# Two transformer layers with a mixture of experts: the last layer norm moved from behind the twelfth expert to beside the eleventh

## The chip, the cores and the metric

The kernel runs on one core of one Trainium2 chip. The metric is the device time of one execution in microseconds (us), median over runs. The profile is one execution taken by the hardware profiler; its times count from the start of its span. Engines: PE is TensorE (matmuls; PEld is its weight load), DVE is VectorE, ACT is ScalarE, POOL is GpSimd, SP is SyncE, which here only issues DMAs. Each engine works through its own instructions in order.

## The reference

Four sub-layers on x of 4 x 1024 rows of 256 float32, each followed by a residual sum and a layer norm: attention with 16 heads, a gated feed-forward network, causal attention with 8 heads, and a mixture of 16 experts. Only the last of them and its norm matter for this change:

```python
logits = xn @ router_weight.T + router_bias
gate_vals, expert_idx = top_k(softmax(logits), 2)
# each expert takes at most CAP = 512 rows, in token order; rows over that are dropped
dispatch = zeros((16, CAP, 256)).at[e_flat, slot].add(xn[tok] * keep)
h = gelu(einsum('ech,efh->ecf', dispatch[4:], fc1) + fc1_bias)     # 12 experts with an MLP, 1024 wide
out_mlp = einsum('ecf,ehf->ech', h, fc2) + fc2_bias
# expert 0 gives zero, 1 its input, 2 and 3 a constant vector
combined = (expert_out[e_flat, slot] * w).sum over the 2 choices / gate_sums
x = layernorm(x + combined)
```

A row of the result therefore has its sum complete only when both experts that chose it are through, and a norm of a row needs the whole sum.

## The kernel before

Everything up to the experts is written out in one hand-made order: the block under `tc.manual_schedule()`, opened at the top and closed by `ordered.close()` (L1457), in which each engine gets its instructions in the order in which the program records them. From L1457 on the planner of the tile framework orders the instructions itself, by its own estimates of when inputs are there.

Tokens are held as 32 tiles of 128 rows (NT = 32, P = 128). Two DRAM tensors carry the mixture of experts. `disp_d` has 512 slots of 260 floats for each of the 12 MLP experts: 256 values of a row, then its expert, its two weights and its token's place, written by indirect DMAs on POOL. Empty slots hold zeros and a place from N = 4096 upwards. `acc_d` has 4096 + 512 rows of 256 floats: the residual plus what the cheap experts give is written there first (`base`, L872), and each MLP expert then adds its rows by an indirect DMA with addition (L1512); the 512 rows at the end take the empty slots. Row p of tile t lies in `acc_d` at place p * 32 + t, so one partition of the last stage reads four tiles as one run of 4 KB.

The loop over the 12 experts e (L1467 on) does for each: load the expert's 512 rows `dm` (four chunks of 128; `load_rows`, on SP's queue, after all rows of all tokens are sent); weights `w` of the rows (L1478, L1479); 8 transposes into `dmT` (L99, copies L100); first matmul `ph` in four PSUM pieces of two buffers (L1492) with the Gelu into `hTm` on ACT (L1500); second matmul `py` in four chunks c (L1508, two PSUM buffers); bias and weight on DVE into `yo` (L1509, L1510); scatter with addition into `acc_d` (L1512). Weights `f1`, `f2` have two buffers each and `load_expert` (L1376 and L1378) fetches them two experts ahead: f1 on SP's queue, f2 on ACT's.

When the last scatter has landed, the last norm begins. SP loads the 4096 rows as eight groups `xo` of four tiles (L1532, 512 KB each). For each group DVE takes the moments (`bn_stats`, `bn_aggr`, L1557 and L1558), POOL the inverse root (`inv_std`, L105 and L106) and the shift `sho` (L1561, L1562), ACT normalises three tiles (L1544) and DVE one (`normalise`, L110), and SP stores the group to `out` (L1550; the last group in two halves, L1548).

Of the kernel before, what the change touches and what calls it, by code (L numbers as in the profile page):

```python
# [19 lines left out]
P = 128  # L20
B, S, C = 4, 1024, 256
N = B * S
NT = N // P
# [12 lines left out]
def postln_layers_kernel(ctx: ExitStack, tc: tile.TileContext, a: dict, out: bass.AP):  # L36
# [29 lines left out]

    disp_d = dram.tile([NSLOT + 2 * N, ROW], F32, name="disp_d")
    acc_d = dram.tile([N + CAP, C], F32, name="acc_d")
    acc_rows = acc_d[0:N, :].rearrange("(p t) d -> p t d", t=NT)


    before = const.tile([P, P], F32, name="before")
# [8 lines left out]
    eidx = const.tile([P, E], F32, name="eidx")  # L81
    nc.vector.tensor_copy(eidx, eidx_i)
    tok_i = const.tile([P, NT], I32, name="tok_i")
    nc.gpsimd.iota(tok_i, pattern=[[1, NT]], base=0, channel_multiplier=NT)
    none_f = const.tile([P, 2, NT], F32, name="none_f")
    for k in range(2):
        nc.vector.tensor_scalar_add(none_f[:, k], tok_i, float(NSLOT + k * N))
# [21 lines left out]
    def normalise(x, mean, rs):  # L109
        nc.vector.tensor_scalar(x, x, mean, rs, ALU.subtract, ALU.mult)  # L110

    with ExitStack() as main:
# [614 lines left out]
        def dispatch(b, big, part=None):  # L727
# [20 lines left out]
            def choose(k):  # L748

                assert (b, (first + n) // 2 - 1) in routed  # L750
                lg = logits()
                if k == 0:
                    t = late_tile(b, [P, 2, ROW], F32, "xn", 12, f"oh_{name}").rearrange("p i d -> p (i d)")
# [83 lines left out]

            def staged(i):
                if ("st", i) not in v:
                    v["st", i] = late_tile(b, [P, 2, ROW], F32, "xn", 12, f"row_{name}_{i}")  # L840
                return v["st", i]

            def row(t):
# [610 lines left out]
        load_rows(0, dm0)  # L1454
        for step in sums3[1:] + sums:
            step()
        ordered.close()  # L1457


    ps_big = ctx.enter_context(tc.tile_pool(name="ps_ph", bufs=2, space=PSUM))  # L1460
# [2 lines left out]
    mo = ctx.enter_context(tc.tile_pool(name="mo", bufs=1))  # L1463


    added = [[]]
    rows = [dm0]  # L1467
    for e in range(EM):
        f1, f2 = loaded[e]
        dm = rows[e]  # L1470
        dmT = mo.tile([P, 2, CAP], F32, tag="dmT", bufs=2, name=f"dmT_{e}")
        hT = mo.tile([P, FF1 // P, CAP], F32, tag="hTm", bufs=2, name=f"hTm_{e}")
        if e + 1 < EM:
            rows.append(mo.tile([P, ECH, ROW], F32, tag="dm", bufs=2, name=f"dm_{e + 1}"))
            load_rows(e + 1, rows[-1])

        w = mo.tile([P, ECH], F32, tag="w", bufs=2, name=f"w_{e}")
        nc.vector.scalar_tensor_tensor(w, dm[:, :, C], float(e - EM), dm[:, :, C + 1], ALU.is_equal, ALU.mult)  # L1478
        nc.vector.tensor_tensor(w, w, dm[:, :, C + 2], ALU.add)  # L1479
        for c in range(2):  # L1480
            transpose_to(
                dmT[:, c, :].rearrange("p (n q) -> p n q", n=ECH),
                lambda i: dm[:, i, c * P : (c + 1) * P],
                ps_m,
                f"ptd_{e}_{c}",
                nc.any.tensor_copy if e else nc.scalar.copy,
            )
        for f in range(0, FF1 // P, 2):
            ph = ps_big.tile([P, S], F32, tag="big", name=f"ph_{e}_{f}")
            for i in range(2):  # L1490
                for c in range(2):
                    nc.tensor.matmul(  # L1492
                        ph[:, i * CAP : (i + 1) * CAP],
                        f1[:, c, (f + i) * P : (f + i + 1) * P],
                        dmT[:, c, :],
                        start=c == 0,
                        stop=c == 1,
                    )
            for i in range(2):
                nc.scalar.activation(  # L1500
                    hT[:, f + i, :], ph[:, i * CAP : (i + 1) * CAP], AF.Gelu, bias=b1[:, e, f + i : f + i + 1]
                )
        yo = mo.tile([P, ECH, C], F32, tag="yo", bufs=2, name=f"yo_{e}")
        added.append([])
        for c in range(ECH):
            py = ps_av.tile([P, 512], F32, tag="av", name=f"py_{e}_{c}")
            for f in range(FF1 // P):
                nc.tensor.matmul(py[:, :C], hT[:, f, c * P : (c + 1) * P], f2[:, f, :], start=f == 0, stop=f == FF1 // P - 1)  # L1508
            nc.vector.tensor_tensor(yo[:, c, :], py[:, :C], b2[:, e, :], ALU.add)  # L1509
            nc.vector.tensor_scalar_mul(yo[:, c, :], yo[:, c, :], w[:, c : c + 1])  # L1510

            ins = nc.gpsimd.indirect_dma_start(  # L1512
                out=acc_d,
                out_offset=bass.IndirectOffsetOnAxis(ap=dm[:, c, C + 3 : C + 4].bitcast(I32), axis=0),
                in_=yo[:, c, :],
                in_offset=None,
                compute_op=ALU.add,
            )
            for other in added[e + 1]:
                tc.declare_no_dep(ins.ins, other, reason="different rows")  # L1520
            for other in added[e] if e else based:
                tc.add_manual_dep(ins.ins, other.name, must, reason="the same rows")
            added[e + 1].append(ins.ins)
        if e + 2 < EM:
            loaded.append(load_expert(e + 2, nc.scalar))


    GRP = 4
    xo = []
    for t0 in range(0, NT, GRP):  # L1530
        x = mo.tile([P, GRP, C], F32, tag="xo", bufs=NT // GRP, name=f"xo_{t0}")
        ins = nc.sync.dma_start(x, acc_rows[:, t0 : t0 + GRP, :])  # L1532
        for other in added[EM]:
            tc.add_manual_dep(ins.ins, other.name, must, reason="all experts' rows")
        xo.append(x)
    done = []

    def finish(x, mv, rs, sh, t0):
        last = t0 + GRP == NT
        for t in range(GRP):  # L1540
            if t == GRP - 1 or (last and t % 2):
                normalise(x[:, t], mv[:, t, 0:1], rs[:, t : t + 1])
            else:
                nc.scalar.activation(x[:, t], x[:, t], AF.Identity, bias=sh[:, t : t + 1], scale=rs[:, t : t + 1])  # L1544
            if t % 2 and last:
                lo = t0 + t - 1
                eng = nc.sync if t == 1 else nc.scalar
                eng.dma_start(out[lo * P : (lo + 2) * P, :].rearrange("(t p) d -> p t d", p=P), x[:, t - 1 : t + 1])  # L1548
        if not last:
            nc.sync.dma_start(out[t0 * P : (t0 + GRP) * P, :].rearrange("(t p) d -> p t d", p=P), x)  # L1550

    for k, x in enumerate(xo):
        t0 = k * GRP
        mv = mo.tile([P, GRP, 2], F32, tag="mvo", bufs=4, name=f"mvo_{t0}")
        for t in range(GRP):
            st = mo.tile([P, 6], F32, tag="bnst", bufs=4, name=f"st_o_{t0 + t}")
            nc.vector.bn_stats(st, x[:, t])  # L1557
            nc.vector.bn_aggr(mv[:, t], st)  # L1558
        rs = inv_std(mo, mv[:, :, 1], GRP, f"o_{t0}")
        sh = mo.tile([P, GRP], F32, tag="sho", bufs=4, name=f"sho_{t0}")  # L1560
        nc.gpsimd.tensor_scalar(sh, mv[:, :, 0], -1.0, None, ALU.mult)  # L1561
        nc.gpsimd.tensor_tensor(sh, sh, rs, ALU.mult)  # L1562
        done.append((x, mv, rs, sh, t0))
        if len(done) > 1:
            finish(*done.pop(0))
    finish(*done.pop())


def _arrays(i):
# [61 lines left out]
```

## Time and profile before

| | |
|---|---|
| runs | 2420.87, 2433.54, 2437.45 us; median 2433.54 us |
| profiled execution | 2424.9 us, span 2423.2 us |
| mean granted TensorE clock | 0.967 |
| PE busy | 2300.8 us, 95% of the span |
| DVE, ACT, POOL busy | 1380.2, 1019.7, 737.5 us |
| DMA | 107.78 MB, 44 GB/s over the span |
| experts, first `ph` to last `py` | 2038.73 to 2388.26 us |
| behind the last `py` | 2388.26 to 2423.2 us |

The last row is the stage that the change is about; the row above it is the stage into which work is moved. Busy shares are means over the whole span, in which these two stages are 16%, so they say little about either.

### The profile page before, as it was taken

The numbers are of one execution on the slowest core, as the hardware profiler recorded it, in microseconds if no ns is written. First come the engines' busy times: TensorE is split into PE (matmuls) and PEld (weight loads), VectorE is DVE, ScalarE is ACT, GpSimd is POOL, SyncE is SP. The second block draws the span as 40 slices with busy tenths as digits, with TensorE's granted clock in tenths as the row PEclk, the third lists the DMA queues.
The fourth block names the chain that finished last, engine by engine and source line by source line (L and its number), as shares of the span: only waits on it lengthen the run. The fifth ranks groups of instructions, "written<-read, shape, count | busy, mean of one in ns | idle before, by whom it ended". The sixth has DMA issues, their size and how long they took to land.

```text
span 2423.2 us, 36155 instructions
## 1 busy us (share of the span) xinstructions
PE 2300.8 (95%) x14004; PEld 1138.6 (47%) x14004; DVE 1380.2 (57%) x3231; ACT 1019.7 (42%) x2039; POOL 737.5 (30%) x1101
## 2 busy tenths in 40 slices
PE   8999999999999999999999999999999985999994
PEld 5333334444444443444444434445556443666662
DVE  7766766666557476776674767717645774111113
ACT  2565665555543445545434555562332331111112
POOL 5335337223205143253241420211112153222223
PEclk9999999999999999999999999998999886999997
DMA  3234111000000000000100000112000012444434
GB/s 104 62 120 138 59 59 51 1 28 1 1 28 1 1 1 24 5 27 27 54 1 1 1 1 12 36 46 80 1 1 1 1 58 92 96 107 107 106 88 150
DMA packets 78125, 107.78 MB, mean 44 GB/s; under 512 B 8832, under 2 KB 67200, under 8 KB 76288
## 3 DMA queue, kind: packets, MB, share of 16 engines
q1 hardware_dynamic: 48592, 73.34, 9.3%
q0 software_dynamic: 9984, 14.82, 3.2%
q10 hardware_dynamic: 19376, 17.30, 2.3%
q8 instruction: 110, 1.80, 0.3%
q14 instruction: 63, 0.52, 0.1%
HBM read 66.54 MB, written 38.90 MB: 44 GB/s over the span
## 4 chain that ended last, share of the span: by engine, by line
PE 87%; DVE 8%; DMA 1%; issue 1%; ACT 1%; POOL 1%; SPq 0%; DVEq 0%; POOLq 0%; ACTq 0%
PE sc L491 21%; PE av L509 10%; PE ph L1492 7%; PE py L1508 7%; PE gu L655 7%; PE mx L960 5%; PE sc L1010 4%; PE mx L467 4%; PE p L929 4%; PE dn L671 3%; PE av L1047 3%; PE ppa L589 3%; PE dn L1047 2%; DVE masked L970 2%; PE qk L321 2%; PE pt L458 1%
## 5 line engine op out<-in xcount | busy, mean ns | idle before, releaser
L470 DVE TENSOR_REDUCE part<-mx 128x1 f32<-128x512 f32 x1024 | 655.6, 684 | 305.8 <-PE mx L467 300.8
L500 ACT ACTIVATE pe<-sc 128x512 f32<-128x512 f32 x1024 | 554.2, 596 | 392.4 <-PE mx L467 349.2
L467 PE MATMUL mx<-kT,qT 32*128 32x512 f32 x2048 | 621.6, 637 | 0.2 <-DVE part L470 0.2
L491 PE MATMUL sc<-qT,kT 32*128 32x512 f32 x2048 | 604.3, 637 | 0.0
L491 PEld LDWEIGHTS sc<-qT,kT 32*128 32x128 f32 x2048 | 176.0, 183 | 218.3 <-issue 174.5
L509 PE MATMUL av<-pe,va 128*32 128x512 f32 x2048 | 272.9, 605 | 0.0
L1021 ACT ACTIVATE pe<-sc 128x512 f32<-128x512 f32 (+3 forms) x384 | 157.3, 496 | 202.2 <-PE sc L1010 202.0
L467 PEld LDWEIGHTS mx<-kT,qT 32*128 32x128 f32 x2048 | 186.1, 183 | 33.3 <-issue 16.0
L970 DVE CUSTOM_DVE_ANT_0 masked<-mx,mask_w 128x128 bf16<-128x128 f32 (+3 forms) x256 | 125.4, 490 | 111.7 <-PE mx L960 82.0
L1492 PE MATMUL ph<-dmT,f 128*128 128x512 f32 x384 | 170.4, 602 | 6.8 <-DVE dmT L100 3.5
L1500 ACT ACTIVATE hTm<-ph,b 128x512 f32<-128x512 f32 x96 | 60.8, 684 | 262.2 <-PE ph L1492 262.2
L1508 PE MATMUL py<-f,hTm 128*128 128x256 f32 x768 | 167.7, 379 | 0.0
L1512 POOL DMA_INDIRECT acc_d<-yo,dm x48 | 74.6, 1554 | 287.0 <-DVE yo L1510 243.8
L1508 PEld LDWEIGHTS py<-f,hTm 128*128 128x128 f32 x768 | 145.9, 190 | 25.0 <-issue 5.7
L1024 POOL TENSOR_SCALAR_AFFINE_SELECT pe<-pe 128x256 f32<-128x256 f32 x128 | 51.7, 412 | 313.2 <-ACT pe L1021 311.5
L960 PE MATMUL mx<-kT,qT 32*128 32x512 f32 (+3 forms) x768 | 138.6, 578 | 3.4 <-DVE x L556 2.7
L1509 DVE TENSOR_TENSOR yo<-py,b 128x256 f32<-128x256 f32 x48 | 20.4, 425 | 213.1 <-PE py L1508 213.1
L386 POOL TENSOR_TENSOR ss<-ss,neg_half 128x16 f32<-128x16 f32 x48 | 139.3, 2910 | 0.5
L509 PEld LDWEIGHTS av<-pe,va 128*32 128x32 f32 x2048 | 40.4, 108 | 192.5 <-issue 186.4
L1010 PE MATMUL sc<-qT,kT 32*128 32x512 f32 (+3 forms) x768 | 123.7, 550 | 5.2 <-ACT pe L1021 1.5
L1492 PEld LDWEIGHTS ph<-dmT,f 128*128 128x128 f32 x384 | 72.9, 192 | 97.4 <-issue 86.8
L856 POOL DMA_INDIRECT disp_d<-row,si x48 | 48.4, 1009 | 221.6 <-DVE row L845 215.4
(350 smaller groups left out, 2992.7 us busy)
## 6 DMA issues: line engine op xcount, KB each, us to landing
f<-in_fc SPq DMA_DIRECT2D x14, 1024.0 KB, 5.0
f<-in_fc ACTq DMA_DIRECT2D x10, 1024.0 KB, 5.9
disp_d<-empty ACTq DMA_DIRECT2D x12, 520.0 KB, 3.3
xink<-in_xT SPq DMA_DIRECT2D x24, 256.0 KB, 3.0
qk_d<-xs SPq DMA_DIRECT2D x6, 1024.0 KB, 5.1
xr<-qk_d SPq DMA_DIRECT2D x6, 1024.0 KB, 6.0
dm<-disp_d SPq DMA_DIRECT2D x11, 520.0 KB, 3.6
x<-in_x SPq DMA_DIRECT2D x32, 128.0 KB, 2.7
```

What stands on the lines that cost most here:

```text
L467: nc.tensor.matmul(sc, self.qT[r, t * P : (t + 1) * P], self.kT[r, u * 512 : (u + 1) * 512], start=True, stop=True)
L470: return lambda: nc.vector.tensor_reduce(self.part[:, t, u, h : h + 1], sc, AX.X, ALU.max, negate=True)
L491: nc.tensor.matmul(sc, self.m.kT[r, kt * P : (kt + 1) * P], self.m.qT[r, qb * 512 : (qb + 1) * 512], start=True, stop=True)
L500: nc.scalar.activation(self.pes[i, h // 2][:, h % 2, :], sc, AF.Exp)
L509: nc.tensor.matmul(self.av[32 * h : 32 * h + 32, :], va0[:, kt, 4 * self.g + h, :], self.pes[i, h // 2][:, h % 2, :], start=kt == 0, stop= ...
L655: nc.tensor.matmul(ps[:, i * 256 : (i + 1) * 256], w[:, c, f * P : (f + 1) * P], xT[j][:, c, :], start=c == 0, stop=c == 1,)
L960: nc.tensor.matmul(scs[h][:, :n], qT[r, t * P : (t + 1) * P], kT[r, u * 512 : u * 512 + n], start=True, stop=True,)
L970: nc.vector.tensor_tensor_reduce(masked[:, :n], scs[h][:, :n], mask_w[:, 512 - n :], -1.0, -NEG, ALU.add, ALU.min, part)
L1010: nc.tensor.matmul(scs[h][:, off:], ones_h[r, :] if w else kT[r, kt * P : (kt + 1) * P], (self.m.nmT if w else qT)[r, q], start=w == 0, st ...
L1021: nc.scalar.activation(pe[:, j, off:], scs[2 * hp + j][:, off:], AF.Exp)
L1492: nc.tensor.matmul(ph[:, i * CAP : (i + 1) * CAP], f1[:, c, (f + i) * P : (f + i + 1) * P], dmT[:, c, :], start=c == 0, stop=c == 1,)
L1508: nc.tensor.matmul(py[:, :C], hT[:, f, c * P : (c + 1) * P], f2[:, f, :], start=f == 0, stop=f == FF1 // P - 1)
```

## The change

The norm of all rows no longer waits for the last expert. While expert 10 (the second last) runs, all 4096 rows are loaded from `acc_d`, with the sums of experts 0 to 9 in them, normed and stored to `out`. The rows that experts 10 and 11 still change are then handled apart: each of these two experts gathers its rows from `acc_d` by an indirect DMA into `xl`, adds its own share to them in SBUF, norms the 512 rows there, and scatters the normed rows over `out` (`place`). Expert 10 also adds its rows to `acc_d`, since expert 11 may share tokens with it. So that empty slots do no harm, `fill_empty` puts the row of the expert's first slot (`one`, read from `disp_d` into all partitions) and its place into every empty slot of experts 10 and 11.

Three further edits go with it. Rows lie in `acc_d` at their token's number, t * 128 + p, so that the same index serves `out`; a load of a group is then four runs of 1 KB for each partition. The experts stand in the hand-made order: `ordered.close()` moves to the end, each expert's rows are turned (`turn_rows`) ahead of the last `py` chunk of the expert before it, `load_expert(e + 1)` and `load_rows(e + 1)` stand after the first `ph` piece of expert e, and a small memset stands ahead of each scatter. `dmT` of expert 0 lies in the pool `tail`, whose tag `xn` has 10 buffers and not 12. All copies of `dmT` are on ACT; before, the planner placed them.

```diff
-    acc_rows = acc_d[0:N, :].rearrange("(p t) d -> p t d", t=NT)
+    acc_rows = acc_d[0:N, :].rearrange("(t p) d -> p t d", p=P)
...
-    nc.gpsimd.iota(tok_i, pattern=[[1, NT]], base=0, channel_multiplier=NT)
+    nc.gpsimd.iota(tok_i, pattern=[[P, NT]], base=0, channel_multiplier=1)
...
-                    v["st", i] = late_tile(b, [P, 2, ROW], F32, "xn", 12, f"row_{name}_{i}")
+                    v["st", i] = late_tile(b, [P, 2, ROW], F32, "xn", 10, f"row_{name}_{i}")
...
-        ordered.close()
...
+    def load_result(t0):
+        x = mo.tile([P, GRP, C], F32, tag="xo", bufs=NT // GRP, name=f"xo_{t0}")
+        ins = nc.sync.dma_start(x, acc_rows[:, t0 : t0 + GRP, :])
+        for other in added[EM - 2]:
+            tc.add_manual_dep(ins.ins, other.name, must, reason="the experts' rows")
+        return x
+    def moments(x, mv, name):
+        st = mo.tile([P, 6], F32, tag="bnst", bufs=4, name=f"st_o_{name}")
+        nc.vector.bn_stats(st, x)
+        nc.vector.bn_aggr(mv, st)
+    def statistics(x, t0):
...
+        for t in range(GRP):
+            moments(x[:, t], mv[:, t], t0 + t)
...
+        inv_std(mo, mv[:, :, 1], GRP, f"o_{t0}", rs)
...
+    def finish():
+        x, mv, rs, sh, t0 = normed.pop(0)
+        for t in range(GRP):
+            if t == GRP - 1:
+                normalise(x[:, t], mv[:, t, 0:1], rs[:, t : t + 1])
+            else:
+                nc.scalar.activation(x[:, t], x[:, t], AF.Identity, bias=sh[:, t : t + 1], scale=rs[:, t : t + 1])
+        to = out[t0 * P : (t0 + GRP) * P, :].rearrange("(t p) d -> p t d", p=P)
+        stored.append(nc.sync.dma_start(to, x).ins)
+    def fill_empty(e, dm):
+        one = mo.tile([P, ROW], F32, tag="one", bufs=1, name=f"one_{e}")
+        ins = nc.sync.dma_start(one, disp_d[e * CAP, :].partition_broadcast(P))
...
+        nc.vector.tensor_copy(first, one[:, C + 3 : C + 4].bitcast(I32))
+        nc.vector.tensor_scalar(first, first, float(N - 1), None, ALU.min)
+        nc.vector.tensor_copy(to, dm[:, :, C + 3].bitcast(I32))
+        nc.vector.tensor_scalar(gap, to, float(N), None, ALU.is_ge)
+        for c in range(ECH):
+            nc.vector.scalar_tensor_tensor(
+                dm[:, c, : C + 3], one[:, : C + 3], gap[:, c : c + 1], dm[:, c, : C + 3], ALU.mult, ALU.add
+            )
...
+        return to_i
...
+    def place(e, c):
+        nc.gpsimd.memset(spacer, 0.0)
+        ins = nc.gpsimd.indirect_dma_start(
+            out=out,
+            out_offset=bass.IndirectOffsetOnAxis(ap=to_is[e][:, c : c + 1], axis=0),
+            in_=xls[e][:, c, :],
+            in_offset=None,
+        )
+        for other in stored + placed[-1:]:
+            tc.add_manual_dep(ins.ins, other.name, must, reason="the rows' last form")
+        placed.append(ins.ins)
...
+    turn_rows(0)
     for e in range(EM):
+        if near:
+            xls[e] = mo.tile([P, ECH, C], F32, tag="xl", bufs=2, name=f"xl_{e}")
+            for c in range(ECH):
+                ins = nc.gpsimd.indirect_dma_start(
+                    out=xls[e][:, c, :],
+                    out_offset=None,
+                    in_=acc_d,
+                    in_offset=bass.IndirectOffsetOnAxis(ap=to_is[e][:, c : c + 1], axis=0),
+                )
+                for other in added[e]:
+                    tc.add_manual_dep(ins.ins, other.name, must, reason="the same rows")
+        if last:
+            for c in range(ECH):
+                place(e - 1, c)
+        if near and not last:
+            xo = [load_result(t0) for t0 in range(0, NT, GRP)]
         for f in range(0, FF1 // P, 2):
...
+            if f == 0 and not last:
+                if 0 < e:
+                    loaded.append(load_expert(e + 1, nc.scalar))
+                rows[e + 1] = mo.tile([P, ECH, ROW], F32, tag="dm", bufs=2, name=f"dm_{e + 1}")
+                load_rows(e + 1, rows[e + 1])
+        if e >= EM - 3 and not last:
+            to_is[e + 1] = fill_empty(e + 1, rows[e + 1])
+        if near and not last:
+            for k in range(5):
+                statistics(xo[k], k * GRP)
+                if k:
+                    finish()
...
         for c in range(ECH):
+            if c == ECH - 1 and not last:
+                turn_rows(e + 1)
...
+            if near:
+                x = xls[e][:, c, :]
+                if last:
+                    nc.vector.scalar_tensor_tensor(x, yo[:, c, :], w, x, ALU.mult, ALU.add)
+                else:
+                    nc.vector.tensor_tensor(x, yo[:, c, :], x, ALU.add)
+                mv = mo.tile([P, 2], F32, tag="mvl", bufs=2, name=f"mvl_{e}_{c}")
+                moments(x, mv, f"{e}_{c}")
+                rs = inv_std(mo, mv[:, 1:2], 1, f"l_{e}_{c}")
+                normalise(x, mv[:, 0:1], rs)
+                if last:
+                    place(e, c)
+                elif c < 3:
+                    statistics(xo[5 + c], (5 + c) * GRP)
+        while normed:
+            finish()
+    ordered.close()
```

More of the change, by code (lines that the diff above doesn't have):

```diff
@@ L752, in choose @@
                 if k == 0:
-                    t = late_tile(b, [P, 2, ROW], F32, "xn", 12, f"oh_{name}").rearrange("p i d -> p (i d)")
+                    t = late_tile(b, [P, 2, ROW], F32, "xn", 10, f"oh_{name}").rearrange("p i d -> p (i d)")
                     for i, key in enumerate((("oh", 0), ("oh", 1), "both", "cum")):
@@ L1463, in postln_layers_kernel @@
     mo = ctx.enter_context(tc.tile_pool(name="mo", bufs=1))
+    GRP = 4
+    stored, normed = [], []
+    def load_result(t0):
[8 more added lines that the diff above has]
+        nc.vector.bn_aggr(mv, st)
@@ new lines, in statistics @@
+    def statistics(x, t0):
+        mv = mo.tile([P, GRP, 2], F32, tag="mvo", bufs=NT // GRP, name=f"mvo_{t0}")
+        for t in range(GRP):
+            moments(x[:, t], mv[:, t], t0 + t)
+        rs = mo.tile([P, GRP], F32, tag="rso", bufs=NT // GRP, name=f"rs_o_{t0}")
+        inv_std(mo, mv[:, :, 1], GRP, f"o_{t0}", rs)
+        sh = mo.tile([P, GRP], F32, tag="sho", bufs=NT // GRP, name=f"sho_{t0}")
+        nc.gpsimd.tensor_scalar(sh, mv[:, :, 0], -1.0, None, ALU.mult)
+        nc.gpsimd.tensor_tensor(sh, sh, rs, ALU.mult)
+        normed.append((x, mv, rs, sh, t0))
@@ new lines, in finish @@
+    def finish():
[10 more added lines that the diff above has]
+        ins = nc.sync.dma_start(one, disp_d[e * CAP, :].partition_broadcast(P))
+        for other in sent:
+            tc.add_manual_dep(ins.ins, other.name, must, reason="rows of all tokens")
+        to, gap, away = [mo.tile([P, ECH], F32, tag=n, bufs=1, name=f"{n}_{e}") for n in ("to", "gap", "away")]
+        first = mo.tile([P, 1], F32, tag="first", bufs=1, name=f"first_{e}")
+        to_i = mo.tile([P, ECH], I32, tag="to_i", bufs=2, name=f"to_i_{e}")
+        nc.vector.tensor_copy(first, one[:, C + 3 : C + 4].bitcast(I32))
[6 more added lines that the diff above has]
+            )
+        nc.vector.tensor_scalar(away, to, first, -1.0, ALU.subtract, ALU.mult)
+        nc.vector.tensor_tensor(away, away, gap, ALU.mult)
+        nc.vector.tensor_tensor(to_i, to, away, ALU.add)
+        return to_i
@@ L1466, in postln_layers_kernel, with turn_rows @@
     added = [[]]
-    rows = [dm0]
-    for e in range(EM):
-        f1, f2 = loaded[e]
+    rows, dmTs, ws = {0: dm0}, {}, {}
+    def turn_rows(e):
         dm = rows[e]
[L1471 to L1477, printed above, removed]
+        pool, tag = (mo, dict(tag="dmT", bufs=2)) if e else (tail, {})
+        dmTs[e] = dmT = pool.tile([P, 2, CAP], F32, name=f"dmT_{e}", **tag)
+        ws[e] = w = mo.tile([P, ECH], F32, tag="w", bufs=2, name=f"w_{e}")
@@ L1485, in postln_layers_kernel @@
                 f"ptd_{e}_{c}",
-                nc.any.tensor_copy if e else nc.scalar.copy,
+                nc.scalar.copy,
             )
+    placed = []
+    def place(e, c):
[9 more added lines that the diff above has]
+        placed.append(ins.ins)
+    to_is, xls = {}, {}
+    turn_rows(0)
+    for e in range(EM):
+        last = e == EM - 1
+        near = e >= EM - 2
+        f1, f2 = loaded[e]
+        dm, dmT = rows[e], dmTs[e]
+        hT = mo.tile([P, FF1 // P, CAP], F32, tag="hTm", bufs=2, name=f"hTm_{e}")
+        if near:
[14 more added lines that the diff above has]
+            xo = [load_result(t0) for t0 in range(0, NT, GRP)]
         for f in range(0, FF1 // P, 2):
@@ L1508, in postln_layers_kernel @@
                 nc.tensor.matmul(py[:, :C], hT[:, f, c * P : (c + 1) * P], f2[:, f, :], start=f == 0, stop=f == FF1 // P - 1)
+            w = ws[e][:, c : c + 1]
             nc.vector.tensor_tensor(yo[:, c, :], py[:, :C], b2[:, e, :], ALU.add)
[L1510 to L1565, printed above, removed]
@@ L1566, in postln_layers_kernel @@
-    finish(*done.pop())
+            if not last:
+                nc.vector.tensor_scalar_mul(yo[:, c, :], yo[:, c, :], w)
+                nc.gpsimd.memset(spacer, 0.0)
+                ins = nc.gpsimd.indirect_dma_start(
+                    out=acc_d,
+                    out_offset=bass.IndirectOffsetOnAxis(ap=dm[:, c, C + 3 : C + 4].bitcast(I32), axis=0),
+                    in_=yo[:, c, :],
+                    in_offset=None,
+                    compute_op=ALU.add,
+                )
+                for other in added[e + 1]:
+                    tc.declare_no_dep(ins.ins, other, reason="different rows")
+                for other in added[e] if e else based:
+                    tc.add_manual_dep(ins.ins, other.name, must, reason="the same rows")
+                added[e + 1].append(ins.ins)
```

## The prediction

> **What bounds the kernel now.** I read the chain that ended last first, in order of time, then the windows around its end. The chain is PE for 87% of the span, and from 2038.73 on it is one expert behind the other: 14.0 us of `ph`, 13.8 us of `py`, every 29.0 us. Behind the last `py` it leaves PE for good.
>
> ```profile
> 2038.73 16.37 PE ph L1492 x32
> ...
> 2360.43 14.00 PE ph L1492 x32
> 2374.43 13.83 PE py L1508 x64
> 2389.37 3.80 DMA acc_d<-yo,dm
> 2393.32 4.04 DMA xo<-acc_d
> ```
>
> ```profile
> 2302.00:2331.00 29.00, 28.66 (x106) 19.09 (x104) 4.60 (x13) 5.06 (x8) 6.20 (x4) 1.00 0.44 109
> 2388.30:2423.20 34.90, 0.00 (x0) 0.00 (x0) 17.28 (x75) 12.17 (x23) 14.89 (x33) 0.55 0.73 248
> ```
>
> The columns of a window are PE, PEld, DVE, ACT and POOL busy, the clock, the DMA share and GB/s. During one expert (first row) PE is full and DVE has 24 us free. The tail of 34.9 us (second row) has no PE at all: 5.1 us until the last scatter has landed, 4.1 until the first group is in, 20 of norms, the rest stores. That tail is what the change can win. It would need DVE to fit the norms beside the eleventh expert without PE noticing.
>
> **What comes off and what stays as a tail.** I count from T, the start of `ph` of expert 10 (2331.50 before); the span before ends at T + 91.7. The new tail behind the last `py`, on one chunk: handoff 0.2, bias 0.42, weight and sum 0.48 (the row of L870, the same kind of DVE operation), moments 0.43 and 0.2, inverse root on POOL about 1.0, norm 0.41, handoffs 0.2, an indirect write 2.6 from issue to landing (the row of `disp_d<-row,si`), and the 2.6 us that lie before between the landing of the last store (issued 2417.70, 2.9 to land) and the span's end: 8.5 us in place of 34.9. With no stall the end would be T + 57.8 + 8.5 = T + 66.3, a gain of 25.4.
>
> **The stall that the program order makes.** It is read from where the instructions stand. On SP the eight `xo` loads now stand ahead of three others: f1 of expert 11, `dm` of expert 11 and `one` of expert 11. On DVE `fill_empty(11)`, which waits for `dm` and `one`, stands ahead of all statistics and of all four `yo` of expert 10. So everything that DVE does in expert 10 waits until SP's queue has worked off the 4 MB. Before, `dm` was never behind more than one weight load, and no `yo` stood behind it.
>
> When does `one` land? The last scatter of expert 9 releases the first `xo` load 5.1 us after PE's end (2388.26 to 2393.32), here at T + 5.1. Then these have to pass: `xo` 4.19 MB, f2 of expert 11 on ACT's queue (1.05, issued about T + 5.1 behind the first Gelu pair), four gathers (0.52), f1 (1.05), `dm` (0.53), `one` (0.13): 7.48 MB. Three rows for the rate, and one for the order:
>
> ```profile
> 2395.00:2405.00 10.00, 0.00 (x0) 0.00 (x0) 7.25 (x33) 3.16 (x6) 4.69 (x11) 0.50 1.00 401
> ...
> 2331.50:2333.00 1.50, 1.50 (x4) 0.78 (x5) 0.81 (x2) 0.00 (x0) 1.02 (x1) 1.00 0.78 162
> 2333.00:2334.50 1.50, 1.50 (x5) 0.65 (x4) 0.00 (x0) 0.00 (x0) 0.53 (x1) 1.00 1.04 371
> ```
>
> ```profile
> dm<-disp_d SPq DMA_DIRECT2D x11, 520.0 KB, 3.6
> ```
>
> ```profile
> DMA to landing us min/median/max: 2.4/4.2/9.4
> ```
>
> The first row is the `xo` load in runs of 4 KB (401 GB/s), the third an f2 load in runs of 1 KB once it streams (371), the second its beginning beside a scatter (162). The changed `xo` load has runs of 1 KB, so I take 380 GB/s: 19.7 us. The first `xo` landed 4.06 us after its issue, of which 1.3 are its own bytes, so 2.8 us are fixed. `one` lands at T + 5.1 + 2.8 + 19.7 = **T + 27.6**. By the HBM limit of 358 GB/s for a core (the Trainium skill, "DMA: Bandwidth & Descriptors", Specifications) it would be 20.9 us and T + 28.8; the rows are above that limit, so I stay with them.
>
> One rule decides against the change. The row says that `dm` takes 3.6 us to land; with that alone `one` would be there by T + 15, after its issue and the loads of f2 and the first `xo` that it waits for. The same page of the skill (Queues, rings and completion order) says that each issuing engine owns one ring on each DMA engine and that descriptors are consumed in ring order: then `one` is the last of SP's 7 MB. By the row the kernel would end about 12.6 us earlier than by the rule. The line of the `xo` tile (loads and stores together) speaks for the rule: loads of equal size issued within 4 us land after 2.4 to 9.4 us, each behind the one before. I take the rule.
>
> **From there to the end.**
> - `fill_empty`: 8 small operations at 0.2 (as in the dispatch) and 4 of 0.48: 3.5. T + 31.1.
> - Statistics of five groups with four norms. Before, a group costs DVE 2.2 us (8 groups from 2397.38, the sixth at 2407.77): 10.7. T + 41.8. Only now does the first `yo` of expert 10 run. PE has been standing since T + 21, for both buffers of `py` are full.
> - Three chunks with one group's statistics each. DVE: 0.9 for `yo`, 1.1 for sum and moments, 0.4 norm, 1.8 statistics. But the root waits on POOL, behind the scatter (1.55, the row of L1512) and behind the four POOL operations of the group before (2.1). A chunk so takes 6.9; three 20.6. T + 62.4. PE's 3.5 us per chunk hide in this.
> - ACT's norms of group 7 stand ahead of the Gelus of expert 11: POOL 2.1, ACT 3 x 0.59, so T + 66.3, first Gelu pair 1.27, T + 67.6. `ph` pieces 0 and 1 are long done and pieces 2 and 3 wait for the PSUM buffers.
> - Two `ph` pieces of 3.5, handoffs 0.5, and PE is cold: behind the wait of 18.6 us at 2014 the first `ph` took 16.37 in place of 14.00, so 2.4. T + 77.5. The stalls before that also leave PE cold, but DVE's 6.9 per chunk covers it.
> - `py` 13.84, tail 8.5: **T + 99.8**. That is 8.1 later than before.
>
> **What comes off ahead of T.** At the first expert ACT waits for the base rows' stores:
>
> ```profile
> 2038.09 1.07 ACT L100 COPY dmT<-ptd 128x512 f32<-128x512 f32 x2 [23.43 <-DMA acc_d<-x]
> ```
>
> With `dmT` of expert 0 in `tail` the copy follows the transposes (2035.66), and the Gelus, which now have that wait, come later than 2038.1 anyway: about 2.1. The transposes ahead of the last `py` chunk take the copy out of the chain: the experts' period is 29.03 against 14.00 + 13.83 + 1.04 = 28.87, ten times 0.13 makes 1.3. Together 3.4. The other edits cost nothing by the rows: `fill_empty(10)` ends about 15 us into expert 9, where DVE is idle until the first `py` chunk at 17.4 (without that cover at most 3.5 once); the memsets of 0.12 run while POOL waits for `yo`; base rows and scatters keep runs of 1 KB; 11 tiles in 10 `xn` buffers reuse only the first, long read. Nothing in the rows says that other DRAM places are slower or faster: between -1 and +1.
>
> The gathers have no row. Below: as fast as a plain load, hidden; above: as slow as a scatter with addition (3.8), four of 1.55 to issue, still ready by T + 15. Neither end reaches the path, since DVE first needs `xl` at T + 42. Their share of the DMA engines is in the sum. The scatters of expert 10's normed rows are four in a row at 2.6, each behind the one before and behind all stores, and end just as expert 11's first chunk is through: 0 to 3.
>
> **Sum:** +8.1 - 3.4 = +4.7. Against the profiled execution 2424.9 this is 2429.6; that execution lies 8.6 under the median of the runs, so I add the difference to the median: **2438**. A measurement here tells from no change about 1% (24 us).
>
> **Rivals.**
> - *The queue does not hold `one` back.* `one` at T + 15, all else the same: 12.6 earlier, 2425. For it: the 3.6 us of `dm`. Against it: 9.4 us for the last `xo`. Chance 0.16; still within 1%.
> - *The tail is hidden as meant.* T + 66.3, less 3.4: 28.8 off, 2405. For it: 24 us of DVE free per expert. Against it: DVE's work in expert 10 is 3.5 + 10.7 + 20.6 = 35 us, all behind `one`; it decides only if that work could start by T - 10. Chance 0.06.
> - *The crowded queues run slowly, and it is slower.* Three queues at once in expert 10, the gathers among them, at the 162 GB/s of the second row: 46 us for the 7.48 MB, `one` at T + 54, 26.5 later, 2465. It decides from 190 GB/s down. For it: that row, and scatters that took up to 6.5 us to land beside a weight load where 3.8 is the median. Against it: the 371 in the very next window. Chance 0.13.
> - My forecast 0.65.
>
> **Range.** The unknown rate alone (300 to 450 GB/s) moves `one` by -3 to +5; POOL's order and the cold clock some 3 more; the median moves by 8. With the first rival and part of the third: 2420 to 2462.
>
> **What would show it.** Right: DVE idle from about T - 3 to T + 27 in expert 10, ended by the load of `one`; PE idle some 20 us before the third `py` chunk of expert 10 and again in `ph` of expert 11; a tail of 8 to 9 us. Wrong: `dm` of expert 11 landing by T + 15, or DVE's first statistics before T + 25; or an expert 10 without an idle PE, which would be the hidden tail.

## The result: slower by 0.4%

The changed kernel takes **2439.24 us** (median of 22 runs, 2428.12 to 2447.48), the kernel before 2425.68 us beside it (22 runs). The ratio, estimated from all runs, is 1.0042, 95% interval 1.0024 to 1.0060 (the two medians alone give 1.0056): slower, by less than the 1% that the forecast took as the bound. A second series (e7 below) gave 1.0019 (0.9999 to 1.0039), which can't be told from no change. The runs of each kernel fall into two groups some 10 to 13 us apart, which in the traces differ ahead of the experts, so beside the medians I compare a stage: from the start of the last write of rows into `disp_d` (L856) to the end of the span. It is 394.9 us before and 402.0 after, and 401.7 in e7: **+7**.

Against the forecast of 2438 the total fits, in part by luck. The forecast added 4.7 to 2433.5, the median of three runs of the kernel before; the 22 runs beside the changed kernel have 2425.7, and the change added 10 to 14 us by these runs and 7 by the stage. The parts do not fit as well either: the experts and their start are 9 us shorter where I had 3.4, and the end is 16 us later where I had 8.1.

### The profile page after: what moved, and what is told of

It reads as the page before. It is cut to its first block, busy times and chain, and to the rows that moved or that the text cites. A ratio compares the mean times of both kernels' runs of the same rounds, so it can differ in the third digit from the quotient of the medians.

```text
span 2440.0 us, 36319 instructions
## 1 busy us (share of the span) xinstructions
PE 2314.2 (95%) x14004; PEld 1146.0 (47%) x14004; DVE 1384.5 (57%) x3259; ACT 1031.1 (42%) x2061; POOL 762.2 (31%) x1181
## 4 chain that ended last, share of the span: by engine, by line
PE 86%; DVE 8%; DMA 2%; issue 1%; ACT 1%; POOL 1%; SPq 0%; POOLq 0%; DVEq 0%; ACTq 0%
PE sc L491 20%; PE av L509 10%; PE gu L655 7%; PE ph L1590 6%; PE py L1620 6%; PE mx L960 5%; PE sc L1010 4%; PE mx L467 4%; PE p L929 4%; PE dn L671 3%; PE av L1047 3%; PE ppa L589 2%; PE dn L1047 2%; PE qk L321 2%; DVE masked L970 2%; PE pt L458 1%
## 5 line engine op out<-in xcount | busy, mean ns | idle before, releaser
L1620 PE MATMUL py<-f,hTm 128*128 128x256 f32 x768 | 172.6, 383 | 25.3 <-DVE yo L1622 25.3
L1627 POOL DMA_INDIRECT acc_d<-yo,dm x44 | 69.4, 1576 | 229.9 <-DVE yo L1624 180.2
L856 POOL DMA_INDIRECT disp_d<-row,si x48 | 48.5, 1010 | 220.8 <-DVE row L845 214.6
```

## The profile after

T is again the start of `ph` of expert 10, now 2332.11. First SyncE's queue (the timeline: start, duration, line, tile, count):

```profile
2337.35 11.93 SPq L1471 DMA_DIRECT2D xo<-acc_d  x8
2349.38 1.36 SPq L1376 DMA_DIRECT2D f<-in_fc  x1
2350.84 0.66 SPq L901 DMA_DIRECT2D dm<-disp_d  x1
2351.59 1.36 SPq L1506 DMA_DIRECT2D one<-disp_d  x1
```

The eight loads of the result go out first. `one` is issued at T + 19.5, 14 us behind the first of them. The issues themselves take that long: the view of the tile `xo` has for the eight of them (min/median/max in ns), here and in the kernel before,

```profile
L1471 SPq DMA_DIRECT2D xo<-acc_d x8: 360/1234/2864, 2337.3 to 2347.5; - x8
```

```profile
L1532 SPq DMA_DIRECT2D xo<-acc_d x8: 339/434/737, 2393.3 to 2396.9; - x8
```

The chain that ended last has its flight as one of its longest pieces:

```profile
2351.59 9.27 DMA one<-disp_d
```

VectorE (the same timeline; the bracket is the idle time before the instruction and what ended it):

```profile
2360.88 0.15 DVE L1512 CAST first<-one 128x1 f32<-128x1 int32 x1 [27.76 <-DMA one<-disp_d]
2375.52 0.42 DVE L1622 TENSOR_TENSOR yo<-py,b 128x256 f32<-128x256 f32 x1
2381.04 0.41 DVE L110 TENSOR_SCALAR xl<-xl,mvl,rs_l 128x256 f32<-128x256 f32 x1 [3.58 <-POOL rs_l L106]
2383.51 0.39 DVE L1622 TENSOR_TENSOR yo<-py,b 128x256 f32<-128x256 f32 x1
2388.67 0.41 DVE L110 TENSOR_SCALAR xl<-xl,mvl,rs_l 128x256 f32<-128x256 f32 x1 [3.24 <-POOL rs_l L106]
2391.13 0.39 DVE L1622 TENSOR_TENSOR yo<-py,b 128x256 f32<-128x256 f32 x1
...
2416.54 0.42 DVE L1622 TENSOR_TENSOR yo<-py,b 128x256 f32<-128x256 f32 x1 [11.06 <-PE py L1620]
2423.85 0.41 DVE L110 TENSOR_SCALAR xl<-xl,mvl,rs_l 128x256 f32<-128x256 f32 x1 [5.68 <-POOL rs_l L106]
```

The first row is the stall: 27.8 us of idle VectorE for one row, copied to all partitions. From there the statistics run, and the first `yo` of expert 10 comes at T + 43.4. Then a chunk takes 7.6 to 8.0 us, 3.2 to 3.6 of them a wait for the inverse root of one column on GpSimd. What PE sees of it:

```profile
2345.84 7.07 PE L1620 MATMUL py<-f,hTm 128*128 128x256 f32 x32
2375.99 6.11 PE L1620 MATMUL py<-f,hTm 128*128 128x256 f32 x16 [23.08 <-DVE yo L1622]
2381.94 1.04 PE L99 MATMUL ptd<-ident,dm 128*128 128x128 f32 x8
2383.96 3.72 PE L1620 MATMUL py<-f,hTm 128*128 128x256 f32 x16 [0.98 <-DVE yo L1622]
2387.51 7.03 PE L1590 MATMUL ph<-dmT,f 128*128 128x512 f32 x16
2403.72 9.33 PE L1590 MATMUL ph<-dmT,f 128*128 128x512 f32 x16 [9.17 <-ACT hTm L1598]
2412.88 10.52 PE L1620 MATMUL py<-f,hTm 128*128 128x256 f32 x48
2424.65 3.72 PE L1620 MATMUL py<-f,hTm 128*128 128x256 f32 x16 [1.24 <-DVE yo L1622]
```

Two `py` fill both buffers, PE stands 23 us, and again 9 us in `ph` of expert 11, where the Gelus queue behind the norms on ScalarE. Behind the last `py` (T + 96.3) come 11.6 us to the end.

The gain stands ahead of T, in PE's weight loads from one expert to the next (here from expert 2 to 3):

```profile
2128.60 1.01 PEld L99 LDWEIGHTS ptd<-ident,dm 128*128 128x128 f32 x8
2132.93 0.41 PEld L1590 LDWEIGHTS ph<-dmT,f 128*128 128x128 f32 x2
```

The second row has no bracket: `ph` waits for nothing, since the transposes of the first row are over 4 us earlier and `dmT` is copied during the last chunk of `py`. In the kernel before, the row of the same step reads:

```profile
2128.27 0.30 PEld L1492 LDWEIGHTS ph<-dmT,f 128*128 128x128 f32 x2 [0.58 <-DVE dmT L100]
```

## Experiments

All stage times are from the profiled execution of each kernel. "Start" is from the last write into `disp_d` to the first `ph`; "period" that of an expert behind the first (the first has 31.4 before and 30.5 after); "py" the end of the last `py` and "end" the end of the span, both counted from T; "whole" from the last write into `disp_d` to the end. The ratio is estimated from all runs and is not the quotient of two medians.

| kernel | start | period | py | end | whole | median, ratio to before |
|---|---|---|---|---|---|---|
| before | 10.4 | 29.03 | T+56.7 | T+91.7 | 394.9 | |
| after | 7.8 | 28.42 | T+96.3 | T+107.9 | 402.0 | 2439.24, 1.0042 [1.0024, 1.0060] |
| e1 order only | 8.0 | 28.42 | T+56.1 | T+90.9 | 385.1 | 2411.95, 0.9919 [0.9894, 0.9944] |
| e2 turn late | 7.9 | 28.98 | T+56.8 | T+91.6 | 391.1 | 2429.63, 0.9988 [0.9970, 1.0007] |
| e3 layout only | 10.4 | 29.03 | T+56.7 | T+91.7 | 394.9 | 2427.24, 0.9989 [0.9971, 1.0007] |
| e4 loads first | 7.9 | 28.42 | T+81.3 | T+92.9 | 387.1 | 2418.88, 0.9967 [0.9949, 0.9986] |
| e5 fill late | 7.6 | 28.42 | T+82.0 | T+93.7 | 387.6 | 2419.04, 0.9978 [0.9960, 0.9996] |
| e6 spread | 8.4 | 28.42 | T+70.8 | T+91.7 | 385.7 | 2419.53, 0.9964 [0.9947, 0.9981] |
| e7 after again | 7.4 | 28.42 | T+96.1 | T+107.8 | 401.7 | 2433.60, 1.0019 [0.9999, 1.0039] |
| e8 scatter late | 8.0 | 28.42 | T+66.5 | T+86.3 | 380.5 | 2417.14, 0.9950 [0.9925, 0.9974] |
| e9 no placing of 10 | 7.6 | 28.42 | T+94.9 | T+103.0 | 397.0 | 2435.43, 1.0031 [1.0015, 1.0047] |

The theory: two parts of the change are independent. The order of the experts gains; the norm beside expert 10 costs, because `one` waits at the end of SyncE's queue and everything on VectorE waits for `one`. The rivals are with each run.

### e1: the order without the norm

```diff
     for e in range(EM):
         last = e == EM - 1
-        near = e >= EM - 2
+        near = False
...
-            if not last:
+            if True:
                 nc.vector.tensor_scalar_mul(yo[:, c, :], yo[:, c, :], w)
```

Behind the loop stands the last norm of the kernel before, the rows lie in `acc_d` as before, and `fill_empty` and the placings are left out; the diff is against the changed kernel.

> The changed kernel's order of the experts, early transposes, dmT_0 in the other pool, 10 buffers of xn and the memsets, but the old layout of acc_d and the old last norm at the end. Measured from the last write of rows into disp_d (before: 394.9 us to the end, changed kernel 402.0). My theory after the traces: the order alone is worth 2.5 at the first expert and 0.6 in each of the others, so 394.9 - 2.5 - 6.5 - 1.2 = 384.7 to the end, period of an expert 28.4 (before 29.0), time about 10 below before. Rival, the prediction's sum: 2.1 + 1.3 = 3.4 less, 391.5 to the end, period 28.9. Second rival: the shorter period comes from the traffic of the other layout or from chance in one profile, and this kernel keeps 29.0 and is within 3 of before.

Measured: whole 385.1, period 28.42 in all experts behind the first, end T + 90.9. The theory's 384.7 is met; the prediction's sum (391.5) misses by 6, and the second rival (within 3 of before) by 7. The tail is the old one, 34.8 behind the last `py`. This kernel beats both: 9.8 us less than before by the stage. By its median, of eight runs, it is 20 less.

### e2: the same, with the transposes behind the last chunk

```diff
         for c in range(ECH):
-            if c == ECH - 1 and not last:
-                turn_rows(e + 1)
...
+        if not last:
+            turn_rows(e + 1)
```

> The kernel of e1_order_only, but the rows of the next expert are transposed behind the last chunk of py instead of ahead of it. If the gain of each expert comes from the early transposes (their PSUM copies on ScalarE are then over when ph starts), the period goes from 28.4 to 29.0 to 29.8, some 7 to 15 us over e1 in the eleven experts. If it comes from the hand order of ph and py alone, the period stays within 0.2 of e1's 28.4 and the times are within 2 us.

Measured: 28.98, the period of before but for 0.05, and 6.0 us more than e1 in the whole (I had expected 7 to 15). Moving these eight transposes by one chunk is the gain of an expert; hand order and copies on ScalarE are not. The wait is back, with another engine's name, in the timeline of e2:

```profile
2150.93 0.30 PEld L1587 LDWEIGHTS ph<-dmT,f 128*128 128x128 f32 x2 [0.53 <-ACT dmT L100]
```

The shorter start (7.9) stays in e2, so it doesn't hang on the transposes of the later experts. Which of the other edits makes it was not run apart; in the trace the first copy of `dmT` starts while the transposes still run (2045.20 in the changed kernel), where before it waited for the stores of the base rows.

### e3: the layout alone

```diff
-    acc_rows = acc_d[0:N, :].rearrange("(p t) d -> p t d", t=NT)
+    acc_rows = acc_d[0:N, :].rearrange("(t p) d -> p t d", p=P)
...
-    nc.gpsimd.iota(tok_i, pattern=[[1, NT]], base=0, channel_multiplier=NT)
+    nc.gpsimd.iota(tok_i, pattern=[[P, NT]], base=0, channel_multiplier=1)
```

> The kernel before with one edit: acc_d keeps a token's row at the token's number (pieces of 1 KB in the last loads), as in the changed kernel. My theory: the eight loads of the last norm, bound by the row rate, get 0 to 2 us slower and nothing else moves: 0 to +2 of before. Rival, that the layout costs the part upstream of the experts (accumulating writes at other addresses) or speeds the experts' scatters: the stage from the first write of acc_d to the first expert, or the period of an expert, differs from before by over 0.2 per expert or the time by over 4.

Measured: 394.9 and T + 91.7, as before: neither cost nor gain. The loads do stream more slowly. A window in the middle of them, first before, then e3 (engines, clock, DMA share, GB/s):

```profile
2397.00:2401.00 4.00, 0.00 (x0) 0.00 (x0) 3.43 (x16) 0.00 (x0) 1.62 (x4) 0.50 1.03 421
```

```profile
2406.00:2410.00 4.00, 0.00 (x0) 0.00 (x0) 3.54 (x16) 0.00 (x0) 1.70 (x4) 0.50 1.07 348
```

421 GB/s with runs of 4 KB, 348 with runs of 1 KB. The tail does not feel it, for a group's norm (2.2 us on VectorE and GpSimd) takes longer than its load either way (1.2 and 1.5).

### e4: the small loads ahead of the large ones

```diff
-        if near and not last:
-            xo = [load_result(t0) for t0 in range(0, NT, GRP)]
         for f in range(0, FF1 // P, 2):
...
             to_is[e + 1] = fill_empty(e + 1, rows[e + 1])
+        if near and not last:
+            xo = [load_result(t0) for t0 in range(0, NT, GRP)]
```

> The changed kernel, but SyncE issues the loads of expert 11 (f1, f2, dm, one) ahead of the eight loads xo. My theory: the row one lands last because it sits behind 4 MB on the same queue; issued first it lands about T + 10 (T = first matmul of ph of expert 10), and VectorE then waits for xo instead: the statistics of five groups end about T + 26, the first yo follows there instead of at T + 43.3, and the end is some 15 to 18 us earlier than the changed kernel's T + 107.7, about T + 91; 7 below before by the medians. Rival 1, the order on the queue is not it (the DMA engines share out all that is pending): one still lands after T + 24 and the end moves by under 3. Rival 2, something else holds the end (ScalarE's and GpSimd's work of the norms, or the chain of placed rows): the first yo is early, but the end moves by under half of the 17.

In e4's timeline `one` now lands at T + 12.9, and VectorE's next wait is 0.8 us for the first `xo`:

```profile
2337.89 0.45 SPq L1506 DMA_DIRECT2D one<-disp_d  x1
2338.39 14.15 SPq L1471 DMA_DIRECT2D xo<-acc_d  x8
```

```profile
2345.16 0.15 DVE L1512 CAST first<-one 128x1 f32<-128x1 int32 x1 [11.88 <-DMA one<-disp_d]
...
2350.96 0.43 DVE L1478 BATCH_NORM_STATS2 st_o<-xo 128x6 f32<-128x256 f32 x1 [0.79 <-DMA xo<-acc_d]
2360.70 0.41 DVE L1622 TENSOR_TENSOR yo<-py,b 128x256 f32<-128x256 f32 x1
```

The first `yo` is at T + 28.4 instead of T + 43.4 and the end 15.0 earlier, all of it kept to the end: both rivals fall. The place on the queue is worth 15 us, and it decides the sign, for e4 is faster than before (0.9967). But e4 is still 2.0 us behind e1 in the whole. With the row in time, moving the norm takes 23.2 us off the tail (11.6 in place of 34.8) and makes the last `py` end 25.2 later (T + 81.3, e1 T + 56.1). What e4 gains over before is the order of the experts.

### e5: the same loads, the waiting work later

```diff
         if e >= EM - 3 and not last:
-            to_is[e + 1] = fill_empty(e + 1, rows[e + 1])
+            load_one(e + 1)
+        if e == EM - 3:
+            to_is[e + 1] = fill_empty(e + 1, rows[e + 1])
         if near and not last:
             for k in range(5):
                 statistics(xo[k], k * GRP)
                 if k:
                     finish()
+            to_is[e + 1] = fill_empty(e + 1, rows[e + 1])
```

`load_one` is the load of `one` alone; its place on SyncE's queue is unchanged.

> The changed kernel, its loads in the same order, but VectorE's work of fill_empty for expert 11 stands behind the statistics of the five groups instead of ahead of them. My theory: only the place of the waiting instruction in VectorE's order makes the wait costly. The statistics then run while one is under way and end about T + 22 to T + 25; one is waited for until T + 28.6, fill ends T + 31.4 and the first yo comes there instead of at T + 43.3: about 12 us earlier than the changed kernel at the end. Rival: the statistics wait for xo as long as fill did for one, since xo lands late as well; then the first yo comes after T + 39 and the gain is under 4.

`one` is awaited until T + 28.2, as in the changed kernel, but five groups have been read by then: VectorE's wait for it is 4.2 us, in e5's timeline

```profile
2343.34 0.15 DVE L1516 CAST first<-one 128x1 f32<-128x1 int32 x1 [4.23 <-DMA one<-disp_d]
```

The first `yo` is at T + 31.0 and the end at T + 93.7, 14.2 earlier than the changed kernel (I had expected 12). With e4 this takes the mechanism from both sides: either the row comes earlier or the work that needs it stands later.

### e6: the work spread over both experts

```diff
+            if last:
+                k = 4 + f // 2
+                statistics(xo[k], k * GRP)
+                finish()
+                if f == 2:
+                    gather(e)
...
-            for k in range(5):
-                statistics(xo[k], k * GRP)
-                if k:
-                    finish()
+            xo = [load_result(t0) for t0 in range(0, NT, GRP)]
+        if near and not last:
+            statistics(xo[0], 0)
+        if last:
+            finish()
+            own_rows(e - 1)
...
+            if near and not last and c < 3:
+                statistics(xo[1 + c], (1 + c) * GRP)
+                finish()
...
-                if last:
-                    place(e, c)
-                elif c < 3:
-                    statistics(xo[5 + c], (5 + c) * GRP)
+                place(e - 1, c)
+    for c in range(ECH):
+        place(EM - 1, c)
```

`gather` reads an expert's rows back, and `own_rows` adds and norms expert 10's, with one root for its four chunks.

> The changed kernel's idea with the work spread: loads of expert 11 first, statistics of one group ahead of the first yo of expert 10 and one behind each of yo 0 to 2, groups 4 to 7 in the four pieces of ph of expert 11, expert 10's own rows normed behind that with one root for four chunks, and one placing of expert 10's rows behind each chunk of expert 11, expert 11's four at the end. My theory (VectorE's order ahead of the first yo is the whole loss): PE keeps nearly its pace, first yo near T + 17, py of expert 11 ends about T + 58 to T + 62, the last four placings in a row add some 10 to 14: end T + 72 to T + 78, 30 to 36 below the changed kernel and 14 to 20 below before. Rival, the tail is bound by VectorE's, ScalarE's and GpSimd's sum of work or by the serial placings wherever they stand: the end does not come before T + 88, and the time is within 5 of before.

A miss. `ph` of expert 11 starts 10 us late, and the end is T + 91.7, where the rival had it (its time within 5 of before is not met: 7.4 less by the medians). The timelines of GpSimd, ScalarE and PE in e6, in this order:

```profile
2351.21 1.68 POOL L1644 DMA_INDIRECT acc_d<-yo,dm  x1 [8.16 <-issue]
```

```profile
2355.14 1.58 ACT L1498 ACTIVATE xo<-xo,sho,rs_o 128x256 f32<-128x256 f32 x3 [10.50 <-POOL spacer L1643]
```

```profile
2361.38 15.43 PE L1599 MATMUL ph<-dmT,f 128*128 128x512 f32 x32 [9.86 <-ACT dmT L100]
```

The first scatter of expert 10 stands 8.2 us on GpSimd. The view of the tile `xo` in e6 says for whom ("who waited for it", us and times):

```profile
POOL acc_d L1644: 8.2, 1
```

The scatter adds into `acc_d`, which the eight loads still read. Behind it on the queue stands the next root, behind that ScalarE's norms, behind those the copies of `dmT`. (The memset of `spacer` in ScalarE's row follows a root on GpSimd's queue.) In the changed kernel this wait does not show: its first scatter of expert 10 runs at 2378.35, behind the wait for `one`.

### e7: the changed kernel again

> The changed kernel itself again, on the chip of the three runs beside it. One to T + 28.6, first yo T + 43.3 and end T + 107.7 as in its first trace, each within 1 us: then the stage's times are the program's and not one execution's. From the last write into disp_d to the end 402. If the whole span differs by about 10 from the first trace's 2440.0 with the same 402, that part lies ahead of the experts, in the attention's granted clock.

T + 28.8, T + 43.4 and T + 107.8 where the first trace had T + 28.8, T + 43.4 and T + 107.9; whole 401.7 against 402.0. The span is 2432.1 against 2440.0 with the same stage: the difference lies ahead of the experts.

### e8: e6 with the scatters of expert 10 later

```diff
+            if last and f == 0:
+                add_rows(e - 1, 0)
+                add_rows(e - 1, 1)
+                own_rows(e - 1)
+            if last and f:
                 k = 4 + f // 2
                 statistics(xo[k], k * GRP)
                 finish()
                 if f == 2:
-                    gather(e)
+                    add_rows(e - 1, 2)
+                    add_rows(e - 1, 3)
+            if last and f == 6:
+                finish()
+                gather(e)
...
+            if not near:
+                add_rows(e, c)
-            if near and not last and c < 3:
+            if near and not last:
                 statistics(xo[1 + c], (1 + c) * GRP)
                 finish()
```

`add_rows(e, c)` is the scatter of one chunk into `acc_d`, with its memset.

> The kernel of e6_spread with GpSimd's queue put in another order: the four accumulating scatters of expert 10 stand behind the roots of the norm's first groups (two in the first and two in the second piece of ph of expert 11) instead of one behind each yo; one more group's statistics go ahead of expert 11, expert 10's own rows are normed in the first piece of ph of expert 11, and expert 11's rows are read back in the last piece. In e6 the first scatter stood 8.2 us on GpSimd's queue; with T = first ph of expert 10 ph of expert 11 began at T + 38.5 behind ScalarE's copies of dmT, and the end came at T + 91.7. My theory: the scatter has to wait until the eight loads xo, which read the same acc_d, have landed, and holds the roots behind it, ScalarE's norms behind those, and the copies of dmT behind them. With the scatters later ph of expert 11 begins at T + 28.5 to T + 31, py ends at T + 58 to T + 63, the end is T + 73 to T + 80, 12 to 18 before e6 and 10 or more before e1_order_only (T + 90.9). Rival: the eight placings in a row and the stores they wait for set the end; then ph of expert 11 is early, but the first placing stays near T + 66 and the end moves by under 4.

The theory of e6 holds for expert 10: `ph` of expert 11 begins at T + 29.2, and the `yo` of expert 10 follow each other after 3.1 to 3.4 us instead of the changed kernel's 7.6 to 8.0. The end meets neither forecast: it is 5.4 before e6, where the theory had 12 to 18 and the rival under 4, and T + 86.3 is 6 us later than the late end of what I expected. The rest of the gain goes in expert 11, whose `py` ends at T + 66.5, 10 us later than in e1, and in the tail of 19.8. The rows of expert 11 are read back late (VectorE waits 3.8 us for them), and then the placings stand in a row. From GpSimd's timeline, the first and the last four:

```profile
2395.11 1.12 POOL L1551 DMA_INDIRECT out<-xl,to_i  x1 [0.41 <-issue]
...
2407.13 0.96 POOL L1551 DMA_INDIRECT out<-xl,to_i  x1 [2.09 <-DMA out<-xl,to_i]
2409.79 0.96 POOL L1551 DMA_INDIRECT out<-xl,to_i  x1 [1.59 <-DMA out<-xl,to_i]
2412.48 0.96 POOL L1551 DMA_INDIRECT out<-xl,to_i  x1 [1.62 <-DMA out<-xl,to_i]
2415.87 0.96 POOL L1551 DMA_INDIRECT out<-xl,to_i  x1 [2.32 <-issue]
```

Eight of them take 20.8 us from the first, at T + 60.7, to the last start, and 4.8 follow to the end. e8 has the shortest stage of all, 14.4 us below before and 4.6 below e1; its times and e1's cannot be told apart (0.9925 to 0.9974 and 0.9894 to 0.9944 overlap).

### e9: the changed kernel without the placing of expert 10's rows

```diff
-        if last:
-            for c in range(ECH):
-                place(e - 1, c)
```

> The changed kernel without the four writes that put expert 10's rows, normed in their slots, over the result (it leaves these rows in the form that the norm of all rows gave them). In the changed kernel the first root of expert 11 stood behind these four writes on GpSimd's queue, VectorE waited 5.7 us for it, and the end came 11.7 us after the last py. My theory: the writes in a row are a cost of the tail: without them the wait falls to about 1.0, the last three chunks follow PE, and the end is T + 102 to T + 104 instead of T + 107.7 (4 to 6 less). Rival: the first chunk's wait is filled by PE's lateness anyway, or the four writes of expert 11 alone set the end; then the end moves by under 1.5.

The end is T + 103.0, 4.9 earlier, and 8.1 us behind the last `py` instead of 11.6. The root's wait in e9's timeline is gone, as expected:

```profile
2413.51 0.41 DVE L110 TENSOR_SCALAR xl<-xl,mvl,rs_l 128x256 f32<-128x256 f32 x1 [1.01 <-POOL rs_l L106]
```

The placings of one expert side by side were not tried: several empty slots write the same row of the result, and unchained the writes would overlap.

## Why the prediction was right, and where only its sum was

| step | predicted | measured |
|---|---|---|
| `one` lands | T+27.6 | T+28.8 |
| empty slots filled | T+31.1 (3.5) | T+31.6 (2.8) |
| first `yo` of expert 10 | T+41.8 (10.7) | T+43.4 (11.8) |
| three chunks done | T+62.4 (6.9 each) | T+66.6 (7.7 each) |
| PE goes on in `ph` of expert 11 | T+67.6 | T+71.6 |
| `py` of expert 11 starts | T+77.5 | T+80.8 |
| last `py` ends | T+91.3 (13.8) | T+96.3 (15.5) |
| end | T+99.8 (8.5) | T+107.9 (11.6) |
| gain at the first expert | 2.1 | 2.6 |
| gain of ten experts | 1.3 | 6.5 |
| sum | +4.7 | +7.1 |

- **The stall was read rightly.** The order on the queue, not the 3.6 us to landing that `dm` usually takes, says when `one` is there: so said the rule of consumption in ring order that I took from the Trainium skill ("DMA: Bandwidth & Descriptors", Queues, rings and completion order), and e4, where `one` goes out first, bears the order out. The trace splits the delay otherwise than I had thought. Most of it, 14.2 us, passes before `one` is issued, while SyncE works through its earlier issues, and 9.3 are its flight; no run tells whether that flight is long by the ring order or by the load on all queues. The sum comes out since it counted bytes, and they had to pass either way. (SyncE's own queue has 5.9 of the 7.48 MB, not 7; and the 2.4 us in the line of `xo` is a store, the loads land after 4.0 to 9.4.) Of the two rates the page's was nearer. I took 380 GB/s from loads of longer runs and from a full stretch of 1.5 us; the changed kernel's loads run at 349, in windows of 6 us

```profile
2338.00:2344.00 6.00, 6.00 (x15) 2.66 (x14) 0.00 (x0) 2.53 (x4) 3.92 (x4) 1.00 1.03 349
2344.00:2350.00 6.00, 6.00 (x25) 4.43 (x24) 0.00 (x0) 1.26 (x2) 0.00 (x0) 1.00 1.08 348
```

  and `one` lands at T + 28.8, which was the estimate by 358 GB/s; before the change, with runs of 4 KB, the loads went above that limit (421), and e3, where the layout alone differs, is under it. The first rival's gain (12.6 for a row that isn't held back) is what e4 makes real: 15.0.
- **The gain of an expert was five times my figure.** The failing term is "14.00 + 13.83 + 1.04 = 28.87, ten times 0.13". These rows are of pipelined matmuls, and neighbouring rows overlap: in the changed kernel 13.90 + 10.52 + 1.04 + 3.62 make 29.08 in a period of 28.42. So their sum hid most of the gap. The weight loads' row of before, 0.58 for `dmT`, had it: e2 brings it back with 0.53, and the period with it.
- **The chunk on VectorE** takes 7.7 and not 6.9. I had put the root behind the right things; the wait for it is 3.2 to 3.6 where my sum left 2.7.
- **The tail** was 8.5 and is 11.6. I gave the placing of expert 10's rows 0 to 3 and took 0. It holds the first root of expert 11 back by 5.7 on GpSimd's queue, so three chunks run behind PE; e9 measures 4.9 with it in all, and its tail of 8.1 is the chunk that I worked out.
- **The two misses have opposite signs**, 5.7 and 8.1, and with a median of before that was 8 us too high that is why 2438 looks as good as it does. With the right terms the same sum gives +7, and 2433 from the 22 runs of before.
- **The hidden tail** had the right condition ("only if that work could start by T - 10"), and e6 and e8 show that it is not enough: in e8 VectorE's work of expert 10 fits in beside PE, but then the rows of expert 11, read back late, and the placings in a row take the place of the tail. The sum had 25.4 us in it; as the last `py` of before ends at T + 56.8, not T + 57.8, its own terms give 26.4. e8 has 5.4 of them.
- **The crowded queues** did not come: `one` would have landed at T + 54.

## What to carry over

Where a small load is needed first, look at what was issued ahead of it on the same queue: one row behind 5.8 MB cost 15 us here, and reordering either the loads or the waiting work gave 14 to 15 back. A period is read from start to start and the gap from the weight loads' row; durations of pipelined matmuls are not added. Work taken off the end by reading and rewriting what is still being written brings its own chain (reads before adds, adds before reads, one write behind the other), and this chain has to be timed like the tail that it replaces. Here the order of the experts alone (e1) did better than the whole change, and of the kernels that move the norm only e8 has a shorter stage.

## What the runs showed besides

The stretch ahead of the experts, with the causal attention in it, moves the whole in the traces: the first write into `disp_d` starts at 1016 to 1021, the last at 2021 to 2040, with nearly the same work to do. The same 50 us, in the changed kernel and in e5 (PE, PEld, DVE, ACT, POOL busy with instructions, the granted clock, DMA share and GB/s):

```profile
1850.00:1900.00 50.00, 48.97 (x296) 26.74 (x296) 22.90 (x79) 13.53 (x33) 5.31 (x13) 0.73 0.00 1
```

```profile
1850.00:1900.00 50.00, 49.26 (x336) 26.71 (x336) 27.87 (x90) 15.32 (x38) 6.46 (x16) 0.90 0.00 1
```

PE is busy in both, but 296 matmuls at a clock of 0.73 stand against 336 at 0.90. The spread is larger than most differences looked for here. What sets the clock there stays open. The indirect writes were the other surprise: one behind the other they start 2.7 to 3.4 us apart, in e8 with PE done and VectorE nearly so.
